# A hybrid block of scan, attention and routed experts: scores and mixing of a bank as one step in five attention batches, and three smaller edits

## The chip, the cores and the metric

The kernel runs on one core of one Trainium2 chip. The metric is the device time of one execution in microseconds (us); the time given for a kernel is the median of its runs. Engines are named as in the profile: PE (TensorE, its matmuls; PEld its weight loads), DVE (VectorE), ACT (ScalarE), POOL (GpSimd), SP (SyncE, which issues transfers).

## The reference, cut to what matters

Eight sequences of 512 tokens with 256 features, all float32, pass through four residual layers: a scan, a mixture of experts, an attention layer and the same mixture of experts again.

```python
x = x + scan(layernorm(x))        # xi = silu(x @ Win + b); h = 0.9*h + xi*Bp; y = (C.h + D*xi) @ Wout
x = x + ffn(layernorm(x))         # mixture of experts, first time
x = x + attention(layernorm(x))   # causal, 16 heads of 16
x = x + ffn(layernorm(x))         # mixture of experts, second time

# attention
scores = clip(q @ k.T * SCALE, -10, 10) + causal_mask
out = softmax(scores) @ v

# ffn
scores = sigmoid(x @ router_w.T)          # 16 experts
topk_idx, tw = grouped_top4(scores)       # 2 of 4 groups, then 4 experts; weights from scores
y = sum over chosen experts of tw * (silu(x @ gate_w[e]) * (x @ up_w[e])) @ down_w[e]
sh = silu(x @ sh_gate_w) * (x @ sh_up_w) @ sh_down_w   # shared experts, all tokens
return y + sh
```

## The kernel before

The program has four stages: a scan stretch over the batches 0 to 7, the routed experts of the first mixture, an attention stretch over the batches 0 to 7, and the routed experts of the second mixture with the final sums.

**A stretch.** A stretch interleaves, batch by batch, several pieces of work: the main work of batch b (scan or attention), the norm and the transposes of the next batch, the routing of batch b−1 (norm, transposes, logits, score, choice of experts, scatter of the rows) and the shared experts of batch b−2. Every piece is a generator that yields the number of PE columns that it has just issued. `beside` walks through the main piece and issues the others as their due times, given as fractions of the main piece's columns, come up (`timed`, `spread`); `behind` fills between. A scheduler then takes the emitted program and fixes a static order of instructions for each engine; `issue_after` sets an instruction behind a given one in PE's order.

**The start.** For batch 0, `first_two` issues load, norm (L412 to L437), transposes on PE (L397) with a copy of each half out of PSUM by ACT (L399), and the input projection (L500, `pz`). In the scan, ACT computes a sigmoid (L509), DVE multiplies (L510) and scans (L512), ACT scales (L513), DVE adds (L516). Batch 1 starts with the same transposes and copies (`xT_l`), while batch 0 is scanned. `layer.copies` of the scan are ACT copies for both halves; `by_both` is ACT for the first half and DVE for the second. POOL adds a bias at L487.

**An attention batch.** Sixteen heads make four groups of four heads (o, w). The scores of one group come in three banks: key tile 0, key tiles 3 and 1, and key tile 2. For each bank, `weights` issues the score matmuls (L1096, `ps_a`, 32 rows of the array each) into two pairs of PSUM banks, an exp by ACT (L1107) and the clamps to the mask by DVE (L1110, L1118). `mix` multiplies such a bank with the values (L1131, `po_a`, 32 columns of the array each), one group later than the scores. `share` copies the result (L1144), transposes it (L1147, `pto_a`) and divides by the sums (L1149, L1150, `o_a`). The output projection is L454 (`py_a`). In `steps`, each bank is two steps: the scores yield, and then the mix of the group before yields. Whole-array work can be issued between any two steps: q and k (L1041, L1052), v (L1059), the shared experts (L958, L987, and tanh at L972), the routing's transposes (L397) and logits (L590, `pl`).

**Routing.** The logits go through a sigmoid on ACT (L599) to the score, also in attention, where all other ACT functions are in one table with exp. DVE chooses the experts in small instructions (L605 to L649). Two matmuls (L656, L657, `pr`) count the rows sent to each expert ahead of each row, DVE turns the counts into places (`row`, L659 to L667), ACT casts them to `slots` (L703), and POOL scatters the rows (L706). `PICKS` is the number of steps of the choice, and `SENT` is how many scatters of batch 6 are issued in the last batch.

**Routed experts.** `run` loads rows for a block of 128 and, in `fetch`, copies its gate weights by ACT and its up weights by DVE (L851) out of a large weight tile `w_all`, at an offset that comes from a register (L816). `turn` transposes the rows (L858) and ACT copies them (L859); then come the hidden layer (L869, `ph`), the activation (L877 to L879), the gain (L882, L890), the way down (L897, L905) and a scatter-add by POOL (L906). Rare extra blocks stand under an If (L936, L939), which is skipped with this data, ahead of the likely blocks.

Of the kernel before, what the change touches and what calls it, by code (L numbers as in the profile page):

```python
# [10 lines left out]
FP = mybir.dt.float32  # L11
# [4 lines left out]
P = 128  # L16
# [58 lines left out]
def tile_hybrid_block(  # L75
# [302 lines left out]
    def issue(piece):  # L378
        for _ in piece.steps:
            pass  # L380
# [204 lines left out]
    def logits(i: int, b: int, tag: str, held):  # L585
        xnT = held["xnT"]
        pl = bank([P, NT, E], f"pl_{tag}")
        for t in range(NT):
            for k in range(KD):
                nc.tensor.matmul(  # L590
                    pl[:, t, :],
                    lhsT=xnT[:, k, t * P : (t + 1) * P],
                    rhs=rw_sb[:, k, :],
                    start=(k == 0),
                    stop=(k == KD - 1),
                )
            yield
        score = small.tile([P, NT, E], FP, tag="score", name=f"score_{tag}")
        nc.scalar.activation(score, pl, AF.Sigmoid)  # L599
        held["score"] = score  # L600

    def choices(i: int, b: int, tag: str, held, paced: bool):
# [50 lines left out]

        pr = bank([P, 2, NT, E], f"pr_{tag}")
        flat = sel.rearrange("p t e -> p (t e)")
        nc.tensor.matmul(pr[:, 0].rearrange("p t e -> p (t e)"), lhsT=tri, rhs=flat, start=True, stop=True)  # L656
        nc.tensor.matmul(pr[:, 1].rearrange("p t e -> p (t e)"), lhsT=ones, rhs=flat, start=True, stop=True)  # L657
        row = small.tile([P, NT + 1, E], FP, tag="row", name=f"row_{tag}", bufs=3)
        nc.vector.tensor_copy(row[:, 0, :], counts[i])  # L659
        for t in range(NT):  # L660
# [145 lines left out]
    def routed(i: int, table, beside):  # L806
# [39 lines left out]
        def fetch(n: int):  # L846


            for half, (copy, name) in enumerate(((nc.scalar.copy, "gate"), (nc.vector.tensor_copy, "up"))):
                here = work.tile([P, KD * F], FP, tag="col", name=f"{name}_{i}_{n}", bufs=COLS)  # L850
                copy(here, w_all[:, bass.ds(held[n][0] + half * KD * F, KD * F)])  # L851
                held[n].append(here)

# [159 lines left out]
    class Attention:  # L1013
# [60 lines left out]
        def main(self, b: int, made):  # L1074
            q_sb, k_sb, v_sb = made
            tag = f"a{b}"
            held = {}

            def weights(o: int, w: int, i: int, at):


                tiles, cols = BANKS[i]
                ps, es = [], []
                for two in range(2):
                    name = f"{tag}_{o}_{w}_{i}_{two}"
                    ps.append(bank([P, 2, T], f"ps_{name}", "pair"))
                    if cols == T:
                        es.append(spot("es", 2))
                    else:
                        es.append(work.tile([P, 2, cols], FP, tag="col", name=f"es_{name}", bufs=COLS))  # L1090
                col = 0
                for c in tiles:
                    n = T - c * P
                    for j in range(HG):
                        r = slice(32 * j, 32 * j + 32)
                        nc.tensor.matmul(  # L1096
                            ps[j // 2][:, j % 2, col : col + n],
                            lhsT=k_sb[w][r, o, c * P : (c + 1) * P],
                            rhs=q_sb[r, o, c * P : T],
                            start=True,  # L1100
                            stop=True,
                        )
                        at[c, j] = es[j // 2][:, j % 2, col : col + n]
                    col += n
                mixed = len(tiles) * P
                for two in range(2):
                    nc.scalar.activation(es[two], ps[two][:, :, 0:cols], AF.Exp, scale=ATT_SCALE)  # L1107
                    diagonal = es[two][:, :, 0:mixed]
                    limit = causal[:, 0 : len(tiles), :].rearrange("p c q -> p (c q)")
                    nc.vector.scalar_tensor_tensor(  # L1110
                        diagonal,
                        diagonal,
                        LOW,
                        limit.unsqueeze(1).to_broadcast([P, 2, mixed]),
                        ALU.max,
                        ALU.min,
                    )
                    nc.vector.tensor_scalar(es[two][:, :, mixed:], es[two][:, :, mixed:], LOW, TOP, ALU.max, ALU.min)  # L1118
                return T + (len(tiles) - 1) * T

            order = [c for tiles, _ in BANKS for c in tiles]

            def mix(o: int, w: int, i: int, at):


                if i == 0:
                    at["po"] = bank([P, T], f"po_{tag}_{o}_{w}")
                for c in BANKS[i][0]:
                    for j in range(HG):
                        h = 8 * o + 2 * j + w  # L1130
                        nc.tensor.matmul(  # L1131
                            at["po"][32 * j : 32 * j + 32, c * P : T],
                            lhsT=v_sb[:, c, h * VC : h * VC + 32],
                            rhs=at[c, j],
                            start=(c == order[0]),
                            stop=(c == order[-1]),
                            tile_position=(0, 32 * j),
                        )
                return len(BANKS[i][0]) * T

            def share(o: int, w: int, at):

                oT = work.tile([P, T], FP, tag="col", name=f"oT_{tag}_{o}_{w}", bufs=COLS)
                nc.scalar.copy(oT, at["po"])  # L1144
                pt = bank([P, NT, HG, 32], f"pto_{tag}_{o}_{w}")
                for t in range(NT):
                    nc.tensor.transpose(pt[:, t].rearrange("p j c -> p (j c)"), oT[:, t * P : (t + 1) * P], ident)  # L1147
                rec = small.tile([P, NT, HG], FP, tag="rec", name=f"rec_{tag}_{o}_{w}")
                nc.vector.reciprocal(rec, pt[:, :, :, DK])  # L1149
                nc.vector.tensor_mul(  # L1150
                    held["o"].rearrange("p t (o j w c) -> p t o j w c", o=NO, j=HG, w=2)[:, :, o, :, w, :],
                    pt[:, :, :, 0:DK],
                    rec.unsqueeze(3).to_broadcast([P, NT, HG, DK]),
                )

            def steps():
                held["o"] = kb4(f"o_{tag}")
                groups = [(o, w, {}) for o in range(NO) for w in range(2)]
                last = None
                for o, w, at in groups:  # L1160
                    for i in range(len(BANKS)):
                        yield weights(o, w, i, at)
                        if last is not None:
                            yield mix(*last[0:2], i, last[2])
                    if last is not None:
                        share(*last)
                        yield T // 2
                    last = o, w, at
                for i in range(len(BANKS)):
                    yield mix(*last[0:2], i, last[2])  # L1170
                share(*last)
                yield T // 2
                yield from turned(lambda: held["o"], f"o{tag}", lambda oT: held.update(oT=oT), by_both)
                yield from add_projection(b, lambda c: held["oT"][:, c, :], wo_sb, KD, tag)

            each = 2 * NT * T + T // 2
            return Piece(2 * NO * each + KD * T // 2 + NT * KD * D, steps())
# [58 lines left out]
    def stretch(layer):  # L1236
# [12 lines left out]
        def turn(b: int, copies=layer.copies):  # L1249
            return turned(lambda: xn.pop(b), f"l{i}_{b}", lambda xnT: xT.update({b: xnT}), copies)  # L1250
# [11 lines left out]
        for b in range(layer.ahead):  # L1262
            if b < layer.early:
                if b in unturned:
                    issue(Piece(0, unturned.pop(b)))
                xT[b] = ready.pop(b)
            else:
                layer.load(b)
                first = i == 0 and b == 0
                issue(Piece(0, norm(b, first)))  # L1270
                issue(Piece(0, turn(b)))
                if first:
                    load_shared()
            if b == 0:
                issue(project(b))
# [24 lines left out]
        for b in range(1 if begun else 0, B):  # L1300
# [19 lines left out]
            if b > 0:  # L1320
# [7 lines left out]
                if last:  # L1328
                    pieces += [
                        timed(r.scores(), *layer.last_scores, *spread(0.5, 0.56, NT)),  # L1330
                        timed(some(r.rest, PICKS), *spread(0.57, 0.7, PICKS)),
                        timed(some(r.rest, 3 + SENT), 0.72, 0.74, 0.76, *spread(0.78, 1.0, SENT)),
                    ]
                else:
                    pieces += [
# [181 lines left out]
```

## Time and profile before

| | |
|---|---|
| median of three runs | 1783.7 us (1783.02 to 1783.77) |
| the profiled execution, its own time | 1759.74 us |
| its span | 1758.0 us |
| mean PE clock granted | 0.981 |
| scan stretch | 0 to 358 us |
| routed experts, first | 359 to 751 us |
| attention stretch | 766 to 1331 us |
| routed experts, second, and final sums | 1334 to 1758 us |

The profiled execution is one execution on its own; its own time is its span and 1.74 us around it. The profile's page lists busy time of each engine, the waits say which instruction waited on which engine's result and for how long, the timeline lists groups of instructions in order of time with the idle time ahead of each and what ended it, and the stretches give busy time by engine in windows of time. Instruction groups are named by the line in the kernel before, the engine, the operation, and output and input tiles.

### The profile page before, as it was taken

The numbers are of one execution on the slowest core, as the hardware profiler recorded it, in microseconds if no ns is written. First come the engines' busy times: TensorE is split into PE (matmuls) and PEld (weight loads), VectorE is DVE, ScalarE is ACT, GpSimd is POOL, SyncE is SP. The second block draws the span as 40 slices with busy tenths as digits, with TensorE's granted clock in tenths as the row PEclk, the third lists the DMA queues.
The fourth block names the chain that finished last, engine by engine and source line by source line (L and its number), as shares of the span: only waits on it lengthen the run. The fifth ranks groups of instructions, "written<-read, shape, count | busy, mean of one in ns | idle before, by whom it ended". The sixth has DMA issues, their size and how long they took to land. (4 is left out here: it accounts for less than half of the span.)

```text
span 1758.0 us, 32867 instructions
## 1 busy us (share of the span) xinstructions
PE 1675.9 (95%) x10640; PEld 1252.9 (71%) x10640; DVE 1100.0 (63%) x3428; ACT 806.7 (46%) x1740; POOL 769.8 (44%) x674
## 2 busy tenths in 40 slices
PE   6899998999999999999999999999999999999993
PEld 3566665589999999944545545545468999999993
DVE  8878877445556655556776576666653655565562
ACT  3222322145555555545654464454423555555551
POOL 3355555535555655420032331322552555455663
PEclk9999999999999999989999999999999999999997
DMA  5444323445555655531012111122543555666666
GB/s 157 139 166 161 133 91 120 163 90 94 98 94 105 108 96 97 103 63 37 25 39 70 68 61 63 52 74 68 184 148 80 98 96 94 111 128 139 119 125 170
DMA packets 149279, 181.38 MB, mean 103 GB/s; under 512 B 16144, under 2 KB 135984, under 8 KB 149104
## 3 DMA queue, kind: packets, MB, share of 16 engines
q0 software_dynamic: 54720, 82.57, 25.0%
q1 hardware_dynamic: 92576, 92.71, 17.6%
q10 hardware_dynamic: 1808, 3.93, 0.6%
q8 instruction: 89, 1.46, 0.3%
q14 instruction: 86, 0.70, 0.1%
HBM read 81.62 MB, written 97.53 MB: 102 GB/s over the span
## 5 line engine op out<-in xcount | busy, mean ns | idle before, releaser
L906 POOL DMA_INDIRECT part<-rows x272 | 426.6, 1568 | 336.8 <-ACT rows L905 244.7
L706 POOL DMA_INDIRECT xg<-sorted_m,slots_m x256 | 256.4, 1002 | 289.5 <-ACT slots_m L703 98.9
L869 PEld LDWEIGHTS ph<-rows,gate 128*128 128x128 f32 x2176 | 285.4, 192 | 21.3 <-ACT rows L859 6.7
L869 PE MATMUL ph<-rows,gate 128*128 128x128 f32 x2176 | 289.4, 276 | 5.1 <-ACT rows L859 5.1
L869 PE MATMUL ph<-rows,up 128*128 128x128 f32 x2176 | 288.7, 276 | 0.0
L897 PE MATMUL pyr<-w_all,rows 128*128 x1088 | 280.5, 380 | 0.9 <-DVE rstd_l L428 0.9
L869 PEld LDWEIGHTS ph<-rows,up 128*128 128x128 f32 x2176 | 266.2, 193 | 0.0
L877 ACT ACTIVATE rows<-ph 128x256 f32<-128x256 f32 x272 | 104.5, 384 | 329.0 <-PE ph L869 329.0
L878 DVE TENSOR_TENSOR rows<-ph,rows 128x256 f32<-128x256 f32 x272 | 115.3, 424 | 193.7 <-ACT rows L877 193.0
L897 PEld LDWEIGHTS pyr<-w_all,rows 128*128 128x128 f32 x1088 | 185.2, 191 | 15.2 <-ACT rows L905 1.3
L851 ACT COPY gate<-w_all 128x512 f32 x272 | 170.0, 626 | 15.2 <-PE ph L869 2.4
L1107 ACT ACTIVATE w_all<-ps_a 128x1024 f32<-128x1024 f32 x128 | 124.4, 1021 | 82.6 <-PE ps_a L1096 77.5
L851 DVE COPY up<-w_all 128x512 f32 x272 | 119.4, 439 | 31.7 <-PE ph L869 17.1
L905 ACT ACTIVATE rows<-pyr,gain 128x256 f32<-128x256 f32 x272 | 128.6, 473 | 15.3 <-PE pyr L897 13.7
L1096 PE MATMUL ps_a<-w_all 32*128 32x512 f32 (+3 forms) x1024 | 123.3, 477 | 7.5 <-ACT w_all L1107 6.4
L958 PE MATMUL pg_m<-xT_m,sg_sb 128*128 128x512 f32 x256 | 124.8, 610 | 0.0
L882 DVE SCALAR_TENSOR_TENSOR gain<-rows,expert_b 128x4 f32<-128x4 f32 x272 | 61.1, 225 | 100.2 <-ACT rows L905 83.5
L958 PE MATMUL pg_m<-xT_m,su_sb 128*128 128x512 f32 x256 | 123.4, 604 | 0.0
L879 DVE TENSOR_TENSOR rows<-ph,rows 128x256 f32<-128x256 f32 x272 | 115.2, 423 | 8.3
L987 PE MATMUL pd_m<-sd_sb,act_m 128*128 128x256 f32 x512 | 119.8, 382 | 0.0
L987 PEld LDWEIGHTS pd_m<-sd_sb,act_m 128*128 128x128 f32 x512 | 95.5, 190 | 20.9 <-issue 4.7
L858 PE MATMUL pt<-ident,rows 128*128 128x128 f32 x544 | 103.7, 273 | 2.9 <-PEq L816 1.0
(219 smaller groups left out, 2215.5 us busy)
## 6 DMA issues: line engine op xcount, KB each, us to landing
rows<-xg SPq DMA_DIRECT2D x272, 136.0 KB, 2.6
part<-x SPq DMA_DIRECT2D x16, 512.0 KB, 3.0
part<-ys_m SPq DMA_DIRECT2D x14, 512.0 KB, 3.0
w_all<-in_L_ffn_gate_w_dram SPq DMA_DIRECT2D x24, 256.0 KB, 5.2
w_all<-in_L_ffn_up_w_dram SPq DMA_DIRECT2D x24, 256.0 KB, 5.8
w_all<-in_L_ffn_down_w_dram SPq DMA_DIRECT2D x24, 256.0 KB, 5.7
sum<-part POOLq DMA_DIRECT2D x10, 512.0 KB, 4.0
xg<-zeros SPq DMA_DIRECT2D x34, 136.0 KB, 2.2
```

The lines of the kernel that those rows point to most:

```text
L706: nc.gpsimd.indirect_dma_start(out=xg[i], out_offset=bass.IndirectOffsetOnAxis(ap=slots[:, at : at + 1], axis=0), in_=rows[:, t, :], in_of ...
L851: copy(here, w_all[:, bass.ds(held[n][0] + half * KD * F, KD * F)])
L869: nc.tensor.matmul(ph[:, s, f * P : (f + 1) * P], lhsT=both[s][:, k * F + f * P : k * F + (f + 1) * P], rhs=rows[:, ROW + k * P : ROW + (k ...
L878: nc.vector.tensor_mul(act, ph[:, 0, :], act)
L879: nc.vector.tensor_mul(act, ph[:, 1, :], act)
L897: nc.tensor.matmul(py, lhsT=act[:, f * P : (f + 1) * P], rhs=w_all[:, bass.ds(w + 2 * KD * F + f * D, D)], start=(f == 0), stop=(f == KF - 1),
L905: nc.scalar.mul(rows[:, 0:D], py, gain[:, TK : TK + 1])
L906: nc.gpsimd.indirect_dma_start(out=parts[i][n % 2], out_offset=bass.IndirectOffsetOnAxis(ap=rows[:, D + 2 * TK : D + 2 * TK + 1].bitcast(U ...
L958: made = nc.tensor.matmul(dst, lhsT=w[:, k, f * P : (f + 1) * P], rhs=xnT[:, k, :], start=(k == 0), stop=(k == KD - 1),)
L987: nc.tensor.matmul(py[:, j, :], lhsT=acts[n][:, f, t * P : (t + 1) * P], rhs=shared[n][3][:, f, :], start=(n == 0 and f == 0), stop=(n == ...
L1096: nc.tensor.matmul(ps[j // 2][:, j % 2, col : col + n], lhsT=k_sb[w][r, o, c * P : (c + 1) * P], rhs=q_sb[r, o, c * P : T], start=True, st ...
L1107: nc.scalar.activation(es[two], ps[two][:, :, 0:cols], AF.Exp, scale=ATT_SCALE)
```

## The change

In attention batches 2 to 6, the scores of a bank and the mix of the same bank of the group before are one step (`close`), so that nothing is issued between them. In attention, the score is computed from exp: exp(−x) on ACT, then a minimum and an addition of 1, and a reciprocal, on DVE; the scan stretch keeps the sigmoid. Both halves of the weights of the first routed block are copied by DVE into a tile of another pool, and, because these copies read registers that must be loaded first, they and the register loads stand ahead of the skipped If in the built order. In the last batch the picks of batch 6 are due at 0.57 to 0.67 and 0.76 instead of 0.57 to 0.70, the steps behind them at 0.79 and later instead of 0.72 and later, and the two counting matmuls of batch 6 are set behind the latest wide instruction (`wide[-1]`). In the first scan batch, the second transposed half is copied by DVE.

```diff
@@ logits
         score = small.tile([P, NT, E], FP, tag="score", name=f"score_{tag}")
-        nc.scalar.activation(score, pl, AF.Sigmoid)
+        if i == 0:
+            nc.scalar.activation(score, pl, AF.Sigmoid)
+        else:
+
+            nc.scalar.activation(score, pl, AF.Exp, scale=-1.0)
+            nc.vector.tensor_scalar(score, score, 3.0e38, 1.0, ALU.min, ALU.add)
+            nc.vector.reciprocal(score, score)
@@ choices
-        nc.tensor.matmul(pr[:, 0].rearrange("p t e -> p (t e)"), lhsT=tri, rhs=flat, start=True, stop=True)
-        nc.tensor.matmul(pr[:, 1].rearrange("p t e -> p (t e)"), lhsT=ones, rhs=flat, start=True, stop=True)
+        with tc.issue_after(wide[-1].ins) if b == B - 2 else nullcontext():
+            nc.tensor.matmul(pr[:, 0].rearrange("p t e -> p (t e)"), lhsT=tri, rhs=flat, start=True, stop=True)
+            nc.tensor.matmul(pr[:, 1].rearrange("p t e -> p (t e)"), lhsT=ones, rhs=flat, start=True, stop=True)
@@ fetch
+            if n == 0:
+
+                both = xpool.tile([P, NT, D], FP, tag="x", name=f"both_{i}").rearrange("p t d -> p (t d)")
             for half, (copy, name) in enumerate(((nc.scalar.copy, "gate"), (nc.vector.tensor_copy, "up"))):
-                here = work.tile([P, KD * F], FP, tag="col", name=f"{name}_{i}_{n}", bufs=COLS)
+                if n == 0:
+                    here = both[:, half * KD * F : (half + 1) * KD * F]
+                    copy = nc.vector.tensor_copy
+                else:
+                    here = work.tile([P, KD * F], FP, tag="col", name=f"{name}_{i}_{n}", bufs=COLS)
                 copy(here, w_all[:, bass.ds(held[n][0] + half * KD * F, KD * F)])
@@ attention steps
+                close = 1 < b < B - 1
                 last = None
                 for o, w, at in groups:
                     for i in range(len(BANKS)):
-                        yield weights(o, w, i, at)
+                        columns = weights(o, w, i, at)
+                        if last is not None and not close:
+                            yield columns
+                            columns = 0
                         if last is not None:
-                            yield mix(*last[0:2], i, last[2])
+                            columns += mix(*last[0:2], i, last[2])
+                        yield columns
@@ stretch, first batches
-                issue(Piece(0, turn(b)))
+                issue(Piece(0, turn(b, by_both if first else layer.copies)))
@@ stretch, last batch
-                        timed(some(r.rest, PICKS), *spread(0.57, 0.7, PICKS)),
-                        timed(some(r.rest, 3 + SENT), 0.72, 0.74, 0.76, *spread(0.78, 1.0, SENT)),
+                        timed(some(r.rest, PICKS), *spread(0.57, 0.67, PICKS - 1), 0.76),
+                        timed(some(r.rest, 3 + SENT), 0.79, 0.81, 0.83, *spread(0.85, 1.0, SENT)),
```

## The prediction

> **What bounds the kernel now.** I read the page's busy shares first, then the stretches (busy time by stage), the waits of PE (TensorE), and the timeline around the places that the diff touches.
>
> ```profile
> PE 1675.9 (95%) x10640; PEld 1252.9 (71%) x10640; DVE 1100.0 (63%) x3428; ACT 806.7 (46%) x1740; POOL 769.8 (44%) x674
> PEclk9999999999999999989999999999999999999997
> ```
>
> PE is busy 95% of 1758.0 us. An edit on DVE, ACT or POOL therefore pays only where PE stands still or runs at a lower clock. The stretches show where that is (columns: stretch, length, busy PE, PEld, DVE, ACT, POOL, PE clock, DMA share, GB/s):
>
> ```profile
> 0.00:40.00 40.00, 23.21 (x59) 12.01 (x60) 32.17 (x72) 13.11 (x20) 14.35 (x51) 0.91 0.56 173
> 363.00:755.00 392.00, 390.81 (x2994) 375.36 (x2994) 227.56 (x721) 214.43 (x539) 209.30 (x136) 1.00 0.58 98
> 819.50:869.50 50.00, 48.05 (x361) 23.61 (x360) 37.76 (x123) 30.29 (x42) 3.23 (x4) 1.00 0.10 33
> 939.90:1008.90 69.00, 68.92 (x429) 35.38 (x428) 46.06 (x146) 34.56 (x56) 21.31 (x20) 1.00 0.19 64
> 1214.60:1270.60 56.00, 49.79 (x352) 23.77 (x351) 41.72 (x135) 28.72 (x47) 22.21 (x23) 0.97 0.45 150
> 1331.00:1345.00 14.00, 11.19 (x65) 10.55 (x66) 5.32 (x18) 5.27 (x13) 0.82 (x1) 0.76 0.43 129
> ```
>
> The first row is the first scan batch: PE lacks work for 16.8 us. The routed block (363–755) has no gap. Attention batch 3 (940–1009) stands for batches 3 to 6, each 69.0 us long: PE is full, so only fewer or shorter PE instructions help. Batch 7 (1214.6–1270.6) leaves 6.2 us. The last row is the entry into the second routed block. PE's largest waits agree (releaser, us in total, times, longest):
>
> ```profile
> PE pr_m L656 <- DVE sel_m L649: 7.1, 3, 3.2
> PE pz_s L500 <- ACT xT_l L399: 7.0, 1, 7.0
> PE ps_a L1096 <- ACT w_all L1107: 6.4, 13, 1.0
> PE ph L869 <- ACT rows L859: 5.1, 4, 2.3
> ```
>
> **What the Trainium skill says.** "TensorEngine Tiling (Array Packing)", Key Properties: a change of tiling mode drains TensorE. This trace agrees and prices it: four pg matmuls (L958, whole array) take 1.82 us from start to next start between neighbours of the same mode and 1.914 with one change beside them; four transposes 0.436 and 0.53. One change costs **0.094 us**. "ScalarE: Activation LUTs", What ACT_TABLE_LOAD costs: about 1283 ns plus a drain of 1380 ns. The load has its 1283 ns here; the drain isn't seen (0.01 us to the next instruction at 852.51). "TensorE: Matmul & The Clock Gate", Part 1, has half clock after idle time, in windows of some 3.4 us. Here PE runs at half clock in pieces of 3.4, 6.8 and 10.2 us, at 26.1–33.0 and 1333.4–1340.3 among others. These follow idle time on PE but are partly chance.
>
> **The change part by part** (minus is a gain).
>
> *Second half of the first transposed batch copied by DVE (L399).* The copy is 0.6 us and is taken off ACT. The larger effect is that the order on DVE changes: the scan steps of batch 0 (L510, L512, channels 0 to 2) now go ahead of the norm of batch 1 (xn, L437), and on ACT L513 goes ahead of the last L509. Before, batch 1 is held by ACT:
>
> ```profile
> 27.56 0.72 ACT L513 ACTIVATE xi_s<-xi_s,d_sb 128x512 f32<-128x512 f32 x1 [1.38 <-DVE state_s L512]
> 28.18 1.05 ACT L399 COPY xT_l<-pt_l 128x512 f32<-128x512 f32 x2
> 28.80 5.75 PE L500 MATMUL pz_s<-xT_l,w_scan 128*128 128x512 f32 x8 [6.95 <-ACT xT_l L399]
> ```
>
> The transposes were ready at 21.8 and their copies stood behind L513 of channel 2. With durations from the trace the new DVE order runs: copy 12.1–12.7, statistics (4 × 0.4 and the small ones) to 15.8, L510 at 16.4, L512 to 18.6, the second pair to 20.8, the third L510 and L512 to 22.8, then xn (2.2) to 25.1. ACT copies at 25.5 and 26.0, PE starts at 26.1 instead of 28.80. DVE's chain of batch 1 begins at 31.9 instead of 33.34, since the last L509 is now late: DVE is the fuller engine of this stage (32.17 of 40), so I count **−1.4**, from −3 (PE's gain in full) to +1.5 (xn delayed by POOL: DVE's small instructions took 0.65 instead of 0.16 us beside POOL's L487).
>
> *Block 0's weights by VectorE ahead of the skip (L851).* Two DVE copies of 0.53 us move ahead of the If; DVE idles 7.08 us there, nothing else waits behind them. ACT still makes three gate copies, of later blocks, ahead of L859 in the built order, so it saves no copy but the register load (0.67 us from 359.36). First entry: **−0.66**, up to +2.9 if a half-clock piece falls there, as one does at the second entry. Second entry: since attention now ends on ACT without the sigmoid's table, one ACT_TABLE_LOAD stands ahead of the gate copies: +1.28 − 0.66 = **+0.6** (0 to +1.3). Before:
>
> ```profile
> 1332.19 1.66 ACT L851 COPY gate<-w_all 128x512 f32 x3 [1.22 <-DMA rows<-xg]
> 1333.76 0.64 ACT L859 COPY rows<-pt 128x256 f32<-128x256 f32 x2
> 1334.17 2.07 PE L869 MATMUL ph<-rows,gate 128*128 128x128 f32 x8 [2.24 <-ACT rows L859]
> ```
>
> *Score from exp in attention (L599).* 15 table loads go; 16 DVE instructions of about 0.2 us come (L605, 128x64: 0.225 us), 3.5 us in all. DVE is busy 46.06 of 69.0 us in batch 3 and has room. Most loads are hidden too, since ACT has 34 us of idle time per batch. In batch 1 two loads delay an exp:
>
> ```profile
> 851.22 1.28 ACT L599 ACT_TABLE_LOAD   x1
> 853.31 1.28 ACT L1107 ACT_TABLE_LOAD   x1 [0.58 <-issue]
> 854.61 1.94 ACT L1107 ACTIVATE w_all<-ps_a 128x1024 f32<-128x1024 f32 x2
> ```
>
> PE then loses 0.45 and 0.90 us around 855 waiting for that exp: **−1.3** (0 if another wait follows). Batches 3 to 6: nothing. In the tail after batch 7 one load leaves the path of the last score and two DVE instructions with their waits enter it: 0, from −1 to +0.5.
>
> *Scores and mixing as one step, batches 2 to 6.* The same matmuls, but the mix (L1131) comes directly behind the scores (L1096) and the whole-array work after both. Counted along PE's built order, mode changes fall from 48 to 43 in each of batches 2 to 5 and from 46 to 41 in batch 6: 25 × 0.094 = **−2.35** (−3.4 to 0). Between two score steps lie the same mix and filler as before, so exp has the same time. In batch 2 the wait of 0.80 us of L1041 for DVE L1052 (883.58) would lie behind a mix: **−0.5** (−0.9 to 0).
>
> *Later picks and counts in batch 7.* PE waits here:
>
> ```profile
> 1254.31 0.64 PE L1131 MATMUL po_a<-es_a,v_a 128*32 128x256 f32 x8
> 1257.93 0.43 PE L656 MATMUL pr_m<-sel_m,tri 128*128 128x64 f32 x2 [2.99 <-DVE sel_m L649]
> 1258.21 0.50 PE L657 MATMUL pr_m<-sel_m,ones 128*128 128x64 f32 x2
> ```
>
> In the built order L656 stands behind three mix groups and a transpose group (L1147), and DVE clamps the last bank before it picks. PE's own work would then end the mix at 1259.3 instead of 1263.1; but DVE's o_a (L1150) comes at 1263.7 by its queue, so the projection starts 2.9 us earlier: **−2.9** (−4.5 to +1). Of what waits for the picks, the scatter (L706) ended at 1320.6 with the routed rows asked for at 1330.39: some 8 us of room. SP's instructions keep their order; POOL moves one memset.
>
> Sum: −1.4 −0.66 +0.6 −1.3 −2.35 −0.5 −2.9 = **−8.5**, made against the profiled execution (1759.74 us, the span and 1.74 around it). The median of the runs is 24.0 above that; I take the same distance: 1783.7 − 8.5 = **1775.2**.
>
> **The rivals.**
> 1. *Half clock goes too* (0.26). At the second entry the first two blocks took 6.56 instead of 3.68 us; batch 7 has another half-clock piece (1258.3–1261.8) that cost about 1.2. Less idling may remove both: −8.5 − 2.9 − 1.2 = −12.6, **1771.1**. Against: the extra table load keeps PE idle at the second entry.
> 2. *The serial chains don't shorten* (0.13). DVE is the next waiter at the start and in batch 7, the exp in batch 1 is bound by its own PSUM bank: only −2.35 − 0.66 + 0.6 = −2.4 is left, **1781.3**.
> 3. *The merged step makes PE wait for exp* (0.09), slower. With the mix at once behind the scores, the next scores could find their PSUM pair not yet read by exp; the wait for L1107 exists already (0.5 us on average, 13 times). Nine merged steps in five batches are 45; at 0.5 us each +22, against −6.2 from the other parts: **1800**. It decides from 0.22 us a step, where it eats 6.2 and adds 3.6. For it: only two PSUM pairs. Against: what lies between the scores is unchanged in sum.
> 4. That the merge doesn't do what it says (order unchanged) is excluded by the built order.
>
> **How the numbers follow.** A measurement of this kernel can tell about 0.2%, 3.6 us: faster is below 1780.1, slower above 1787.3. Forecast 0.52, rival 1 0.26 and a little of rival 2 are faster: 0.80. The rest of rival 2 is the same: 0.11. Rival 3 is slower: 0.09. The range goes from 1769.5 (rival 1 with the start's lower bound) to 1783.5 (rival 2 with a half-clock piece at the first entry), and leaves out rival 3 and the far ends of the unknown costs.
>
> **What would show it.** Right: batches 3 to 5 last 68.5 instead of 69.0 us; pz of batch 1 starts near 26; L656 in batch 7 has no wait near 3 us; the loads at L599 are gone in attention, with one ahead of the gate copies near 1325. Wrong: a batch of 69 us or more, with waits of L1096 for L1107; ph of the second entry more than 1.3 us later after the last pd than before; the first batch's copy waited for by PE.

## The result, and the profile after

The changed kernel takes **1775.8 us** (median of 20 runs, 1771.3 to 1781.5) where the kernel before takes 1783.8 beside it (20 runs, 1778.3 to 1789.2): the ratio is 0.995, with an interval of 0.9939 to 0.9962. The forecast was 1775.2. The profiled execution of the changed kernel took 1771.3 us, its span is 1769.6.

The trace of before that the prediction shows comes from a quicker execution than those run beside the changed kernel: 1758.0 us of span against 1784.7 when the kernel before was profiled again as `before_again`. So I compare traces of one and the same set of runs. Line numbers have moved: L655 was L649, L663 was L656, L865 was L851, L873 was L859, L883 was L869, L972 was L958, L1066 was L1052, L1110 was L1096, L1121 was L1107, L1145 was L1131, L1161 was L1147.

The engines and PE's clock, from the page of the changed kernel:

```profile
PE 1676.6 (95%) x10640; PEld 1252.6 (71%) x10640; DVE 1099.8 (62%) x3447; ACT 789.0 (45%) x1724; POOL 769.4 (43%) x674
...
PEclk9999999999999999999999999999998999999997
```

PE's own work is what it was (1675.9 before). ACT has 16 instructions fewer, DVE 19 more. The stretches that answer to those of before (stretch, length, busy PE, PEld, DVE, ACT, POOL, PE clock, DMA share, GB/s):

```profile
0.00:40.00 40.00, 24.70 (x60) 12.22 (x61) 31.15 (x73) 12.64 (x19) 14.32 (x51) 0.91 0.56 173
370.00:762.00 392.00, 390.66 (x2994) 375.04 (x2993) 227.59 (x720) 214.09 (x538) 208.61 (x136) 1.00 0.56 98
823.60:872.50 48.90, 47.54 (x361) 23.33 (x360) 38.52 (x125) 27.72 (x40) 3.23 (x4) 1.00 0.10 33
942.90:1012.10 69.20, 68.27 (x430) 35.33 (x428) 46.82 (x148) 32.02 (x54) 21.25 (x20) 1.00 0.18 63
1217.10:1273.40 56.30, 52.32 (x352) 23.64 (x351) 41.81 (x137) 26.23 (x45) 19.87 (x21) 0.94 0.45 148
1340.00:1354.00 14.00, 9.63 (x56) 8.76 (x56) 4.32 (x16) 7.24 (x13) 0.82 (x1) 0.76 0.43 129
```

The third row is attention batch 1, a microsecond shorter. The fourth is batch 3, which should have fallen to 68.5 and is 69.2 long: PE is busy 68.27 us of it instead of 68.92 in 69.0, so PE has less to do and waits instead. The waits of PE name what it waits for (releaser, us in total, times, longest):

```profile
PE pt_l L397 <- DVE xn L437: 12.7, 4, 9.8
...
PE ph L883 <- ACT rows L873: 5.5, 3, 3.1
PE pg_m L972 <- ACT expert_b L793: 5.1, 1, 5.1
PE pr_m L663 <- DVE pick_m L647: 4.9, 1, 4.9
PE ps_a L1110 <- ACT w_all L1121: 4.8, 9, 1.0
PE pr_m L663 <- DVE sel_m L655: 4.8, 3, 3.7
...
PE pz_s L500 <- ACT xT_l L399: 2.6, 1, 2.6
...
PE pto_a L1161 <- DVE w_all L1066: 1.7, 2, 0.8
...
PE pto_a L1161 <- ACT slots_m L710: 1.2, 2, 0.6
```

In `before_again` the same answer has 6.4 us for exp (L1121 now), 17.4 for the picks (the two rows of `pr_m` now) and 7.4 for the first copies (`pz_s`), so these fell; the wait for the norm (`xn`) was 9.8 and has risen to 12.7. The last two rows are new. By stage, measured between starts of named PE instructions (an attention batch runs from the last `py_a` of one batch to that of the next), in us; "before" is `before_again` and `merge_alone` (where the merge has no part), "changed" the changed kernel and its repeats `after_again` and `changed_third`:

| stage | predicted | before | changed | mean difference |
|---|---|---|---|---|
| start to first `pz` of scan batch 7 | −1.4 | 262.1, 262.2 | 261.8, 262.1, 260.3 | −0.7 |
| from there to last `pd` of the scan stretch | 0 | 109.2, 108.7 | 103.7, 103.8, 103.3 | −5.3 |
| first entry, `pd` to `ph` | −0.66 | 4.33, 4.33 | 3.82 each | −0.51 |
| attention batch 1 | −1.3 | 50.00, 50.00 | 48.89 each | −1.11 |
| batches 2 to 6 | −2.85 | 345.2 | 344.6 each | −0.6 |
| batch 7 | −2.9 | 61.3, 61.4 | 56.3, 57.3, 57.3 | −4.3 |
| last `py_a` to last `pd` | 0 | 66.7, 66.5 | 66.7, 67.4, 67.0 | +0.4 |
| second entry | +0.6 | 4.18, 4.19 | 5.10 each | +0.92 |

The sum is some 11 us for these single traces, and 8 to 9.5 in the medians; single executions of one kernel differ by 5 us either way. The total came out as predicted, its parts did not all: the merge brought little, and the largest item is at the end of the scan stretch, where nothing was predicted.

### The profile page after: what moved, and what is told of

Read it like the earlier page. It is cut to its first block, busy times and chain, and to the rows that moved or that the text cites. A ratio compares the mean times of both kernels' runs of the same rounds, so it can differ in the third digit from the quotient of the medians.

```text
span 1769.6 us, 32866 instructions
## 1 busy us (share of the span) xinstructions
PE 1676.6 (95%) x10640; PEld 1252.6 (71%) x10640; DVE 1099.8 (62%) x3447; ACT 789.0 (45%) x1724; POOL 769.4 (43%) x674
## 3 DMA queue, kind: packets, MB, share of 16 engines
q8 instruction: 89, 1.46, 0.3%
## 5 line engine op out<-in xcount | busy, mean ns | idle before, releaser
L883 PEld LDWEIGHTS ph<-rows,gate 128*128 128x128 f32 x2160 | 282.4, 192 | 15.5 <-ACT rows L873 1.0
L883 PE MATMUL ph<-rows,gate 128*128 128x128 f32 x2160 | 285.7, 275 | 0.4 <-ACT rows L873 0.3
L883 PE MATMUL ph<-rows,up 128*128 128x128 f32 x2160 | 285.4, 275 | 0.0
L883 PEld LDWEIGHTS ph<-rows,up 128*128 128x128 f32 x2160 | 263.1, 192 | 0.0
L865 ACT COPY gate<-w_all 128x512 f32 x270 | 168.8, 627 | 13.7 <-PE ph L883 2.4
L1121 ACT ACTIVATE w_all<-ps_a 128x1024 f32<-128x1024 f32 x128 | 124.4, 1021 | 78.9 <-PE ps_a L1110 65.4
L865 DVE COPY up<-w_all 128x512 f32 x270 | 119.8, 444 | 29.3 <-PE ph L883 11.9
L919 ACT ACTIVATE rows<-pyr,gain 128x256 f32<-128x256 f32 x272 | 128.7, 473 | 15.1 <-PE pyr L911 13.6
L972 PE MATMUL pg_m<-xT_m,su_sb 128*128 128x512 f32 x256 | 127.2, 619 | 5.2 <-ACT expert_b L793 5.1
L1110 PE MATMUL ps_a<-w_all 32*128 32x512 f32 (+3 forms) x1024 | 122.5, 478 | 6.0 <-ACT w_all L1121 4.8
L972 PE MATMUL pg_m<-xT_m,sg_sb 128*128 128x512 f32 x256 | 123.6, 604 | 0.0
```

Source lines behind the costliest of these rows:

```text
L883: nc.tensor.matmul(ph[:, s, f * P : (f + 1) * P], lhsT=both[s][:, k * F + f * P : k * F + (f + 1) * P], rhs=rows[:, ROW + k * P : ROW + (k ...
L919: nc.scalar.mul(rows[:, 0:D], py, gain[:, TK : TK + 1])
L972: made = nc.tensor.matmul(dst, lhsT=w[:, k, f * P : (f + 1) * P], rhs=xnT[:, k, :], start=(k == 0), stop=(k == KD - 1),)
L1110: nc.tensor.matmul(ps[j // 2][:, j % 2, col : col + n], lhsT=k_sb[w][r, o, c * P : (c + 1) * P], rhs=q_sb[r, o, c * P : T], start=True, st ...
```

## The experiments

They ran in three sets, each on another chip, with runs of the kernel before beside them. The medians of before were 1785.95, 1764.35 and 1786.9 us: the chip of the second set is some 20 us quicker, so times are compared within a set only.

**First set: the repeats, and the merge alone or left out.** `before_again` is the kernel before, `after_again` the changed one.

> The kernel before, unchanged, to see which of its stage times repeat. Theory T (the stage times of the one trace of before are typical): batches 3 to 5 last 69.0 us each, batch 7 56.0, the scan's tail after its last projection 58.4, attention's tail 59.5, and the span is near 1758. Rival U (that one execution was a lucky one by 24 us): the span is near 1782, and the 24 us are in the two tails (some 7 us each, as the trace of after has them) and in half-clock pieces.

> The changed kernel, unchanged, to see which of its stage times repeat. Theory T: the waits of the first trace come again: L1161 for the DVE copy L1066 in batch 3 (0.84 us) and 4, tails of 65 and 66.7 us. Rival U: the tails are a matter of chance and differ by several us from the first trace, while the waits of L1161 are the same to 0.1 us. Time 1775 +- 3, ratio to before 0.995.

Measured: 0.9992 [0.9978, 1.0005] for the kernel before against itself, which shows what a measurement can tell, and 0.9943 [0.9926, 0.9961] for the changed one (1776.4). Rival U of `before_again` came true: its span is 26.6 us longer than that of the first trace of before, of which 13.6 are at the end of the scan, 7.2 in the tail of attention (last `py_a` to last `pd`) and 5.3 in batch 7, while attention batches 1 to 6 are the same to 0.01 us. In `after_again` PE waits 0.87 us for L1066 in batch 3, as in the first trace of the changed kernel.

`merge_alone` is the kernel before with this edit, and `after_no_merge` the changed kernel with `close = False`:

```diff
+                close = 1 < b < B - 1
...
-                        yield weights(o, w, i, at)
+                        columns = weights(o, w, i, at)
+                        if last is not None and not close:
+                            yield columns
+                            columns = 0
                         if last is not None:
-                            yield mix(*last[0:2], i, last[2])
+                            columns += mix(*last[0:2], i, last[2])
+                        yield columns
```

> The kernel before with the merged step of batches 2 to 6 alone. Theory of the prediction: 5 mode changes fewer per batch give 0.47 us in each of batches 2 to 6, so batches 3 to 5 last 68.5 us and the whole is 2.4 us faster (ratio 0.9987). Rival: PE then reaches the transposes L1147 of the first group before DVE has emptied their PSUM bank, because DVE is held by the load of x; the wait of 0.6 to 0.9 us takes the gain, batches 3 to 5 last 68.9 to 69.2 us, and the ratio is 1.000.

> The changed kernel with the scores and mixing as two steps again, all else kept. Theory of the prediction: batches 3 to 5 are 0.47 us longer than in the changed kernel, the whole 2.4 to 2.9 us longer (1778.5). Rival (the gain is eaten by the wait for DVE): batches 3 to 5 last 69.0 us, within 0.2 us of the changed kernel, and the whole is the same 1775 to 1776, so the 8 us come from other parts.

Measured: the merge alone 1786.8, ratio 1.000 [0.9988, 1.0013]; without it 0.9964 [0.9949, 0.9979]. In the traces batches 2 to 6 take 344.6 us with the merge and 345.2 without in the one pair, 344.6 and 344.9 in the other. So the merge is worth 0.3 to 0.6 us, and not 2.85. In whole batches, `changed_third` against `after_no_merge`: batch 2 is 0.36 us longer (70.42 to 70.06), batch 3 0.10 longer, batches 4 and 5 some 0.1 shorter, and batch 6, where PE has no wait, 0.59 shorter (67.23 to 67.82). The rival of a wait for exp is ruled out: in batches 2 to 5 neither `merge_alone` nor `changed_third` has any wait of the scores for exp. What stands there instead is seen in batch 3 of the changed kernel. The timeline of DVE there (start, busy, line, operation, out<-in, count, idle time before and what ended it):

```profile
952.73 0.69 DVE L157 TENSOR_TENSOR x<-x,more 128x512 f32<-128x512 f32 x1 [3.15 <-DMA x<-part]
...
964.11 0.73 DVE L1066 TENSOR_SCALAR w_all<-pq_a,parity 128x512 f32<-128x512 f32 x1
```

and that of PE:

```profile
963.02 1.13 PE L1073 MATMUL pv_a<-w_att,xT_l 128*128 128x256 f32 x4
964.99 0.63 PE L1161 MATMUL pto_a<-ident,oT_a 128*128 128x128 f32 x4 [0.84 <-DVE w_all L1066]
965.45 1.03 PE L1073 MATMUL pv_a<-w_att,xT_l 128*128 128x256 f32 x4
```

and PE at the same place in `before_again`:

```profile
971.16 0.64 PE L1131 MATMUL po_a<-es_a,v_a 128*32 128x256 f32 x8
971.73 1.13 PE L1059 MATMUL pv_a<-w_att,xT_l 128*128 128x256 f32 x4
972.69 0.60 PE L1147 MATMUL pto_a<-ident,oT_a 128*128 128x128 f32 x4
```

PE reaches the transposes 0.84 us sooner than it may write them: they wait for DVE to finish with `pq_a`, a tile of another operation whose place they take. Counted from the batch's start, the transposes begin at 22.33 us in `before_again` and at 22.08 here; without the wait it would be 21.24. Nearly all of this 1.09 us is order and not speed: four groups of v matmuls (L1059, L1073 now) stood ahead of the transposes in this batch before, and three do now; the fourth, 0.96 us of PE's time, has come behind them. Batches 2, 4 and 5 wait at their first transposes too, by 0.5 to 0.9 us, and batch 3 ends 0.15 us longer than before (69.15 to 69.00). DVE comes no sooner than before because its queue still stands 3.15 us at L157, the first addition for the next batch, whose operand is still being loaded; from there to L1066 DVE works without a gap.

**Second set: each of the other edits alone, added to the kernel before.** There are four of them, not three. The hunks are those shown under the change. `late_picks_alone` has the new due times of batch 7 and `issue_after` for the counts; `first_copy_alone` has only `turn(b, by_both if first else layer.copies)`; `block0_alone` the edit in `fetch`; `exp_score_alone` the score from exp.

> The kernel before with the later picks and counts of the last batch alone. The prediction gave this part 2.9 us, all in attention's batch 7. In the repeats, batch 7 lasts 61.3 us before and 56.3 to 57.3 changed, and the end of the scan (from the last projection's start, pz of batch 7, to the last pd) 109 us before and 103.5 changed. Theory 1: this part makes both gains: batch 7 near 57, end of the scan near 103.5, ratio 0.995. Theory 2: it makes batch 7's alone (57; end of the scan stays 109; ratio 0.9975). Theory 3: batch 7's gain needs the exp score as well: 59 or more.

Measured: 1758.6, 0.9976 [0.9963, 0.9989]. Batch 7 lasts 54.75 us, against 57.41 in `block0_alone` and 57.49 in `first_copy_alone`, where it is as before and the mean clock in it is the same 0.94: −2.7. The end of the scan takes some 95 us in all traces of this chip, so what the picks do to the 109 us of the first set could not be seen here.

> The kernel before with the second half of the first transposed batch copied by DVE, alone. Prediction: 1.4 us earlier from the first batch on (pz of batch 2 at 60.3 instead of 61.7), nothing elsewhere. Rival (the end of the scan is 5 us shorter because everything comes a little earlier against POOL's scatters): end of the scan near 104 instead of 109 us, 6.5 us in all.

Measured: 1764.6, 1.0006 [0.9994, 1.0018]. The first `pz` of scan batch 2 came at 59.37, against 61.18 to 62.50 in the three others of the set, but the first of batch 7 at 261.52 against 261.57 to 263.43: the gain at the start is in part taken back in batch 2, and is not seen in the time.

> The kernel before with block 0's weights by DVE ahead of the skipped If, alone. Prediction: 0.66 us off both entries into the routed blocks, since attention then still ends with the sigmoid's table: from the last pd to the first ph 3.8 us instead of 4.33 (first) and 3.6 instead of 4.18 (second). Rival: the register loads ahead of the If also change the end of the scan (109 us) by several us.

Measured: 1762.7, 0.9993 [0.9976, 1.0009], with entries of 3.83 and 3.82 us against 4.34 and 4.19 in `first_copy_alone`: −0.5 and −0.4. The edit itself gains at both entries.

> The kernel before with the score from exp in attention, alone. Prediction: batch 1 1.1 to 1.3 us shorter (48.9 instead of 50.0), batches 2 to 6 as before, the second entry 1.28 us longer for its table load (5.4 instead of 4.18), batch 7 nearly as before (60 to 61.3): in sum 0 to -1. Rival: the score's chain in batch 7 gains by the loads that go (two of 1.28 us), and batch 7 is 2.5 us shorter: sum -2.5.

Measured: 1765.4, 1.0001 [0.9989, 1.0013]. Batch 1 lasts 48.89, as in the changed kernel, so the −1.11 comes from this edit alone. Batch 2 is 0.3 us shorter (70.09) and batch 3 0.15 longer (69.15); the prediction had listed neither. The second entry is 5.47, 1.28 us longer: one table load, whose group has 1283 ns. Batch 7 lasts 58.68, but its mean clock is 0.88 instead of 0.94, so it says nothing of the expected or the rival gain there.

**Third set: the end of the scan, the picks, and the wait of the merge.** `changed_third` is the changed kernel.

> The changed kernel, unchanged, once more. The runs of the kernel before were near 1785 us beside the first experiments and near 1764 beside the last ones, where PE's results were signalled without the delays of 8 to 11 us at the ends of scan and attention. Theory (the change's parts add up to 5 us without those delays: -0.5 first entry, -1.1 batch 1, -0.6 merge, -2.7 batch 7, +0.9 second entry, -1.4 start): beside a kernel before of 1764 the ratio is 0.997; beside one of 1785 it is 0.995. Rival (all of the gain is in the parts that were predicted): 0.995 in both.

Measured: 1779.0, 0.9951 [0.9935, 0.9967]. The kernel before took 1786.9 beside it, so this run can't decide between the two readings: both say 0.995 there. The whole change has not run on the quick chip.

`after_early_picks` is the changed kernel with the old picks:

```diff
-        with tc.issue_after(wide[-1].ins) if b == B - 2 else nullcontext():
+        with nullcontext():
...
-                        timed(some(r.rest, PICKS), *spread(0.57, 0.67, PICKS - 1), 0.76),
-                        timed(some(r.rest, 3 + SENT), 0.79, 0.81, 0.83, *spread(0.85, 1.0, SENT)),
+                        timed(some(r.rest, PICKS), *spread(0.57, 0.7, PICKS)),
+                        timed(some(r.rest, 3 + SENT), 0.72, 0.74, 0.76, *spread(0.78, 1.0, SENT)),
```

> The changed kernel with the picks and counts of the last batch at their old times and place, all else kept. Theory (the later picks make most of the gain): batch 7 is 2.7 us longer than in the changed kernel (60 instead of 57), the ratio to before rises to 0.9985 to 1.000. Where the delays of PE's signals are seen, the end of the scan shows whether it was this part that shortened it (109 us) or not (103.5). Rival (exp and merge bring half of the gain): ratio 0.997 or less.

Measured: 1782.3, 0.9967 [0.9954, 0.9981], which is the rival's ratio; the theory's 0.9985 to 1.000 did not come. Batch 7 of attention is 59.7 instead of 57.3 (PE waits 3.29 us for the picks again, at a clock of 0.89 instead of 0.97), and the end of the scan 105.6 instead of 103.3. These differences are no price of the picks: `after_late_add` below has the later picks and took 59.5 and 105.3 in the same places. In the scan stretch this edit moves no instruction at all; PE, DVE, ACT and POOL each have the same order in both traces.

`after_late_add` takes away what the merge makes PE wait for: the addition with the late load, and the first steps of the norm behind it, fall due later, so that DVE's copy goes ahead.

```diff
-                    pieces.append(timed(added, 0.24, 0.28))
+                    pieces.append(timed(added, 0.33, 0.35))
...
-                    timed(norm(nxt), *spread(0.32, 0.44, NT), *spread(0.56, 0.64, NT)),
+                    timed(norm(nxt), *(spread(0.36, 0.46, NT) if i else spread(0.32, 0.44, NT)), *spread(0.56, 0.64, NT)),
```

> The changed kernel with the addition of the two parts of the next x (DVE, L157) due at 0.33 and 0.35 of a batch instead of 0.24 and 0.28, and the next norm's first steps with it (0.36 to 0.46). It takes away the wait of DVE for the load of x (3.1 us) that stands ahead of the copy L1066 whose PSUM bank the transposes L1161 wait for. Theory (the merge's gain is eaten by that wait): the waits of L1161 for L1066 go (0.84 us in batch 3), batches 3 to 5 last 68.4 to 68.6 us instead of 68.9 to 69.2, 1.5 to 2.5 us in all. Rival (the mode changes cost nothing in the merged order): batches 3 to 5 stay at 68.9 to 69.2 although the wait is gone.

Measured: batches 2 to 5 last 68.67, 68.71, 68.71 and 68.72 us, 274.8 together, against 277.3 in `changed_third`: −2.5. The theory had batches 3 to 5 at 68.4 to 68.6. In this stretch the answer of the waits has no line for PE left; `changed_third` has 3.8 us there, 2.8 of them at L1161. The same transposes as above, on PE, and the stretch of batch 3:

```profile
965.44 0.60 PE L1161 MATMUL pto_a<-ident,oT_a 128*128 128x128 f32 x4
```

```profile
944.40:1013.10 68.70, 68.50 (x430) 35.37 (x428) 47.38 (x148) 32.02 (x54) 19.15 (x20) 1.00 0.19 64
```

They begin 21.07 us into the batch, 1.0 sooner, without a wait. So the wait behind DVE's queue was what ate the merge's gain in batches 3 to 5. In batch 2 the later addition also ends two waits that the kernel before had (0.79 and 0.45 us), and no run has it without the merge, so that batch's gain can't be shared out. The whole kernel took 1778.0, 0.9947 [0.9927, 0.9968]: no better than the changed one beside it by this measurement. Its trace lost 2.2 us in batch 7 (59.5 instead of 57.3) and 2 at the end of the scan, where the order of instructions is that of the changed kernel; so much do single executions differ there. I can't call it a faster version.

`after_scan_counts` moves the counting of the last scan batch back, in the scan stretch only, so that nothing waits for DVE in the middle of the batch:

```diff
-                        timed(some(r.rest, 3 + SENT), 0.79, 0.81, 0.83, *spread(0.85, 1.0, SENT)),
+                        timed(
+                            some(r.rest, 3 + SENT),
+                            *((0.79, 0.81, 0.83) if i else (0.96, 0.97, 0.98)),
+                            *spread(0.85 if i else 0.99, 1.0, SENT),
+                        ),
```

> The changed kernel with the counting matmuls of batch 6 in the scan behind the second half of the last projection (due at 0.96 instead of 0.79; attention as it was), so that PE has work while DVE picks. In the changed kernel PE waits 3.8 to 4.9 us there, and runs at half clock for 6.8 us after. Theory: the wait goes to under 1 us and the half clock with it: end of the scan 4 to 6 us shorter, ratio to the changed kernel 0.997. Rival: the scatters of batch 6 come later by that time and PE waits for them at the first entry: no gain.

Measured: 1786.2, 0.9992 [0.9979, 1.0006]: the whole gain of the change is lost. The end of the scan takes 111.9 us. The wait didn't go; it moved, and not to the first entry, as the rival had it (3.83 us, as in the changed kernel). The timeline of PE and DVE there ("remote": the trace names no engine of this core that ended the wait):

```profile
303.41 4.00 PE L1001 MATMUL pd_m<-sd_sb,act_m 128*128 128x256 f32 x10 [4.60 <-DVE act_m L992]
...
327.35 0.69 DVE L992 TENSOR_TENSOR act_m<-pg_m,sig_m 128x512 f32<-128x512 f32 x1 [5.04 <-remote]
...
331.49 0.66 PE L663 MATMUL pr_m<-sel_m,tri 128*128 128x64 f32 x2 [9.38 <-DVE sel_m L655]
```

## Why the prediction was right or wrong

**The number** was right: 8.5 forecast, 8.0 measured. Its working was right for about half of the sum; two errors, the merge and the end of the scan, point opposite ways.

**The merged step was mis-sized.** The sentence "exp has the same time" held. The term "25 × 0.094 = −2.35" failed, and the price of a change of mode was the smaller part of it: with all waits gone, batches 3 to 5 of `after_late_add` are 0.29 us shorter than before and batch 6 0.59, for 5 changes fewer each: 1.46 for 20, so 0.073 apiece on average instead of 0.094. Why batch 6 gains twice as much as the others is open. What failed above all is that the step reckoned PE's time alone. I named the wait of L1041 in batch 2 and put −0.5 on it, but didn't ask who else takes a tile that DVE L1052 must leave. The merged order brought the transposes of batch 3 ahead by one group of v matmuls, and they met DVE's copy there. In batch 2 the named wait went, three others of 0.3 to 0.8 us came, and the batch grew by 0.36 instead of losing 0.5. In `after_late_add`, where the waits are cured, batches 2 to 6 are 2.8 us shorter than in `after_no_merge` (342.0 to 344.9), about what was forecast, with the later addition's own share in batch 2. This was the second rival's mechanism (DVE is the next waiter) in a stage to which I hadn't applied it.

**Batch 7** went as worked out for the later picks: 2.9 predicted, 2.7 with the edit alone at the same clock. PE's timeline shows the counts behind the mix, and the wait of 2.99 us down to 0.99:

```profile
1261.55 1.93 PE L1145 MATMUL po_a<-w_all,v_a 128*32 128x512 f32 x24
1264.47 0.41 PE L663 MATMUL pr_m<-sel_m,tri 128*128 128x64 f32 x2 [0.99 <-DVE sel_m L655]
```

The rest of the 4.3 us was not separated. The mean clock of this batch is 0.89 in `before_again` and 0.94, 0.97 and 0.97 in the three traces of the changed kernel. Length times missing clock gives 6.7 us lost before and 1.7 to 3.4 after (an estimate), so the first rival's mechanism, less half clock, came true here in part. It is partly chance: the same instructions had 0.91 in `after_late_add`. `after_early_picks` has the 0.89 of the kernel before and is still 1.6 shorter.

**Batch 1** and **the entries** went as worked out. In batch 1, predicted 1.3 and measured 1.11, ACT's timeline has the score between two exps and no load:

```profile
856.50 0.22 ACT L603 ACTIVATE score_m<-pl_m 128x64 f32<-128x64 f32 x1 [1.00 <-PE pl_m L590]
...
857.62 1.94 ACT L1121 ACTIVATE w_all<-ps_a 128x1024 f32<-128x1024 f32 x2 [0.90 <-PE ps_a L1110]
```

A wrong term was hidden there: I took some 0.2 us for each of the 16 added DVE instructions, 3.5 in all, and the reciprocal takes 553 ns, so they are 6.0 us (last columns of the groups: busy, mean ns | idle before):

```profile
L605 DVE RECIPROCAL score_m<-score_m 128x64 f32<-128x64 f32 x8 | 4.4, 553 | 0.3
...
L604 DVE TENSOR_SCALAR score_m<-score_m 128x64 f32<-128x64 f32 x8 | 1.6, 194 | 3.4 <-ACT score_m L603 2.5 <-issue 0.9
```

At the second entry the table load (Trainium skill, "ScalarE: Activation LUTs", What ACT_TABLE_LOAD costs: about 1283 ns; the trace agrees, with 1.28 us) stands on the path as foreseen. With it the entry grew by 0.92 and not by 0.6, since the saving was 0.4 rather than 0.66:

```profile
1341.87 1.28 ACT L865 ACT_TABLE_LOAD   x1 [0.83 <-DVE gain L896]
1343.16 1.66 ACT L865 COPY gate<-w_all 128x512 f32 x3
1344.73 0.64 ACT L873 COPY rows<-pt 128x256 f32<-128x256 f32 x2
...
1345.14 3.14 PE L883 MATMUL ph<-rows,both 128*128 128x128 f32 x13 [3.15 <-ACT rows L873]
```

The first rival also hoped for half clock to go here; PE still waits 3.15 us, and the clock of this stretch is 0.76, as in the first trace of before.

**The start** was right in size as far as batch 2 (−1.4 predicted, −1.9 found) and wrong in its steps. The norm of batch 1 came when I said, but ACT's copies did not come at 25.5:

```profile
22.84 2.20 DVE L437 TENSOR_SCALAR xn<-x,mv_l,rstd_l 128x256 f32<-128x256 f32 x4
...
26.97 0.69 ACT L509 ACTIVATE xi_s<-pz_s,b_in_sb 128x512 f32<-128x512 f32 x1 [3.46 <-DVE y_s L516]
27.55 1.07 ACT L399 COPY xT_l<-pt_l 128x512 f32<-128x512 f32 x2
...
28.19 1.22 PE L500 MATMUL pz_s<-xT_l,w_scan 128*128 128x512 f32 x1 [2.65 <-ACT xT_l L399]
```

The copies stand behind the last L509 on ACT, and that waited 3.46 us for L516 on DVE, behind the norm. The prediction had noted that this L509 would be late, but let the copies start ahead of it. Of the 1.9 us, 0.7 on average was left at batch 7: in `after` and `after_again` PE ran at half clock for 3.4 us near 81, and batch 2 is 1.7 us longer there than in `changed_third`. The first trace of before has such a piece too, at 80.7.

**The end of the scan** is the part that I didn't have at all: −5.3 us. The kernel before loses time there in one wait. Its timeline (`before_again`):

```profile
296.76 0.97 POOL L706 DMA_INDIRECT xg<-sorted_m,slots_m  x1 [0.30 <-issue]
300.11 0.69 DVE L463 TENSOR_TENSOR x<-py_s,x 128x512 f32<-128x512 f32 x1 [9.82 <-remote]
...
302.69 0.69 PE L656 MATMUL pr_m<-sel_m,tri 128*128 128x64 f32 x2 [13.58 <-DVE sel_m L649]
```

PE ended the first half of `py_s` at 289.1. DVE's addition of it began at 300.11, after a wait that the trace puts down to no engine of the core ("remote"); the picks stand behind it on DVE, PE waits 13.58 us for them, and the counts find PE at half clock. In the changed kernel the wait of L463 is short, and on the quick chip (`late_picks_alone`) there is none:

```profile
291.54 0.69 DVE L463 TENSOR_TENSOR x<-py_s,x 128x512 f32<-128x512 f32 x1 [1.64 <-remote]
...
294.11 0.69 PE L663 MATMUL pr_m<-sel_m,tri 128*128 128x64 f32 x2 [4.95 <-DVE pick_m L647]
```

```profile
290.34 0.69 DVE L463 TENSOR_TENSOR x<-py_s,x 128x512 f32<-128x512 f32 x1
...
292.91 0.43 PE L657 MATMUL pr_m<-sel_m,tri 128*128 128x64 f32 x2 [2.61 <-DVE sel_m L649]
```

Up to the end of this batch's work the order of instructions is the same in both kernels, so no moved instruction explains it, nor does the time at which the batch begins: `after_again` reaches it at 262.10, `before_again` at 262.07. The merge isn't it (108.7 alone, 103.1 without). The later picks move no instruction of the scan stretch, and the exp score has none in it. The first copy and block 0's weights are left, and whether one of them makes the difference stays open: alone they ran only on the chip of the second set, where no such wait occurs; there the end of the scan took 94.1 to 95.8 us with each of the four edits. The prediction's base, too, had no such wait (95.6 from the first `pz` of batch 7). So the forecast's sum could not hold this item. On the two slow chips it made up for what the merge failed to bring, and that part of the agreement of the total is luck.

## What to carry to other kernels

When the order on PE is changed, follow each PSUM tile to the engine that frees its place: here one group of matmuls fewer ahead of the transposes was enough for them to meet a place that DVE, held up by a load, freed 0.5 to 0.9 us late, and the gain was lost there. If the total agrees with a forecast, compare the stages before believing the reasons, and take base and changed kernel from the same set of runs. A function that leaves ACT's loaded table costs what stands on the path at the place where the table is next loaded, not its count.

## What the runs showed of the hardware

- On two of the three chips a result of PE was at times seen late by the engine that waited for it. In `before_again` PE ended the first half of `py_s` at 289.1 and L463 was released at 300.1, 11 us later. In the attention tail ACT waited 10.98 us for `pe_b` and DVE 8.19 for `pl_b`; in `late_picks_alone`, on the quick chip, the same waits took 4.22 and 2.41. The changed kernel has these two as well (11.03 and 8.23 in `after`). The first trace of before and the four traces of the second set have no wait put down to "remote".
- In `before_again` these releases came 2.2 to 2.4 us after a run of POOL scatters ended (300.11 after 297.73; 1338.82 after 1336.61), in `after_scan_counts` 2.5 us (327.35 after 324.81), and one short wait (L463 in the changed kernel) ended inside such a run. That scatters hold the signals back is an argument from these times, and no run tried it. Against scatters as the only cause: in `late_picks_alone` 32 of them ran through the same place, from 277.0 to 317.8, and no signal was late.
- One reciprocal of 128x64 on DVE took 553 ns, where a minimum with an addition of that size, in one instruction, took 194.
- The next instruction on ACT after a table load began 0.01 us after the load's end (1343.16 after 1341.87 + 1.28).
- The same kernel had a median of 1764 us on one chip and of 1786 and 1787 on two others.
